# Moving two sets of 128x128 transposes of an attention kernel from TensorE to 32x32 block transposes on VectorE and transfers inside SBUF

## The chip, the cores and the metric

The kernel runs on one core of one Trainium2 chip. The metric is the device time of one execution in microseconds (us). A core has five engines with a queue of instructions each: TensorE (PE, matrix multiplications; its weight loads are shown apart as PEld), VectorE (DVE), ScalarE (ACT), GpSimd (POOL) and SyncE (SP), which here only issues transfers. Every engine works through its queue in order. SBUF is the working memory of 128 partitions, PSUM the memory that TensorE writes its results into.

## The reference

Two layers on 16 graphs of 1024 nodes with 256 features. Only the first layer is touched. Its attention uses the same values as queries, keys and values, in 8 heads of 32 features:

```python
h = jnp.maximum(_layernorm(x, axis=-1), 0.0)
normed = layer_norm(h, gamma1, beta1)
qkv = normed.reshape(b_, n_, H, HD).transpose(0, 2, 1, 3)      # H = 8, HD = 32
scores = jnp.einsum('bhqd,bhkd->bhqk', qkv, qkv) * scale
attn = jax.nn.softmax(jnp.where(mask, scores, -jnp.inf), axis=-1)
out = jnp.einsum('bhqk,bhkd->bhqd', attn, qkv)
out = out.transpose(0, 2, 1, 3).reshape(b_, n_, d_)
h2 = h + out
y = layer_norm(h2, gamma2, beta2)
x = x + h2 + (jax.nn.gelu(y @ W1 + b1) @ W2 + b2)
# second layer: h = relu(layernorm(x)); attention over all features of h,
# with logits h W a_12 W^T h^T + ..., then elu(h W_1 + attention h W_2); x = x + that
```

All of it is computed in float32.

## The kernel before

The batch has 16 graphs; the text calls one graph a batch (b). The whole program is unrolled, and the order of the instructions on every engine is the order in which the program writes them (the last lines of `fast_path` fix it). That order is made by seven streams, each a generator that names the place of its next piece in units of a batch; the loop near line 1487 always takes the earliest piece. `stream_a` writes the attention of batch b at places b to b+1, `stream_c` prepares the values of batch b at b-0.70 to b-0.25, and `stream_b` writes the rest of batch b (the two matrix products of the first layer, then all of the second layer) from b+0.99 on, beside the attention of batch b+1. A clock counts the TensorE time written so far. `defer(us, f)` holds back a piece of another engine until the clock has moved on by that much, so that it stands in its engine's queue where its operands should be ready. `turns` is a list of TensorE transposes that are asked for; `make_turns` writes them at the start of the next unit of attention.

Attention works in units (half of the queries qh, group g of 4 heads, tile kt of 128 keys), 32 to a batch. `scores` multiplies keys by 512 queries, both read from `kT`, a tile with the four heads of a group in the four groups of 32 partitions, features along the partitions and nodes along the columns. Each product has 32 rows and 64 columns of the array, so eight lie side by side. VectorE adds the mask (line 1000), ScalarE takes the exponential (line 1007), and one unit later `weigh` multiplies the values `va` (nodes along the partitions) by it (line 1022). After 8 key tiles the result `o` has head and feature along its partitions and 512 queries along its columns. In batch 0 half of the mask is added by TensorE.

Two sets of transposes are concerned:

- `turn(i)` in `prologue` (line 817): `va` of 256 nodes, nodes along the partitions, becomes `kT`. Four 128x128 transposes on TensorE into the PSUM tile `ptk` (line 822), then one copy by ScalarE (line 825). Four times a batch.
- `finish` (line 951): VectorE copies `o` to `os` (line 1031), TensorE transposes it in four blocks into `ptos` (line 958), VectorE multiplies by the inverse of the softmax sum `rl` (line 960), POOL adds to `h` (line 964). Four times a batch, for each (qh, g). `invert` makes `rl` when all units are done that a half needs.

When `finished` counts both groups of a half, `prepare` may compute the layer norm of two tiles of `h` (statistics on VectorE, a power on POOL at line 744, normalising on VectorE), `turn` in `rest` transposes them (`pty`, line 1143), `expand` multiplies by W1 and `contract` by W2. In `rest`, chunks 0 and 1 belong to the first half of the nodes, 2 and 3 to the second.

SP issues all transfers in the written order: loads of masks (line 585), of x (lines 784 and 1108), transposing transfers of the masks (line 902) and the stores of the output (line 1321).

Of the kernel before, what the change touches and what calls it, by code (L numbers as in the profile page):

```python
# [17 lines left out]
P = 128  # L18
# [477 lines left out]
def fast_path(  # L496
# [54 lines left out]
    ep = pool("ep", 6)  # L551
    denp = pool("denp", 2)
    lp1 = pool("lp1", 6)
# [220 lines left out]
    def prologue(b, st):  # L774
# [42 lines left out]
        def turn(i):  # L817
# [8 lines left out]

        steps = [
# [6 lines left out]
            lambda i: turns.append((1, lambda: turn(i))),  # L834
# [116 lines left out]
    def finish(b, qh, g, rl, ready, os):  # L951
        h = hs[b]
        run_deferred(ready)
        finished[b, qh] = finished.get((b, qh), 0) + 1
        clock[0] += 0.5
        pt = ps_tile([P, TPH, P], f"ptos_{b}_{g}_{qh}")
        for t in range(TPH):
            nc.tensor.transpose(pt[:, t, :], os[:, t * P : (t + 1) * P], ident)
        ot = tmpp.tile([P, TPH, GH, HD], F32, tag="w2", bufs=5, name=f"ot_{b}_{g}_{qh}")
        nc.vector.tensor_mul(  # L960
            ot, pt.rearrange("p t (j d) -> p t j d", d=HD), rl.unsqueeze(3).to_broadcast([P, TPH, GH, HD])
        )
        ho = h[qh][:, :, g * P : (g + 1) * P]
        nc.gpsimd.tensor_add(ho, ho, ot.rearrange("p t j d -> p t (j d)"))  # L964

    def attention(b, st):
        va, kT = st["va"], st["kT"]
        den = denp.tile([P, NQH, NT, H], F32, tag="den", name=f"den_{b}")


        def scores(qh, g, kt):
            qs = slice(qh * QW, (qh + 1) * QW)
# [11 lines left out]
            for j in range(GH):  # L984
                r = slice(j * HD, (j + 1) * HD)
                for c in range(0, P, P // 2):
                    nc.tensor.matmul(  # L987
                        sc[j // 2][c : c + P // 2, j % 2, :],
                        kT[r, g, kt * P + c : kt * P + c + P // 2],
                        kT[r, g, qs],  # L990
                        start=j >= by_pe,
                        stop=True,
                    )
# [23 lines left out]
        def weigh(qh, g, kt, es):  # L1017
            if kt == 0:
                acc[g, qh] = pso.tile([P, QW], F32, tag="o", name=f"o_{b}_{g}_{qh}")
            o = acc[g, qh]  # L1020
            for j in range(GH):
                nc.tensor.matmul(  # L1022
                    o[j * HD : (j + 1) * HD, :],
                    va[:, kt, (g * GH + j) * HD : (g * GH + j + 1) * HD],
                    es[j // 2][:, j % 2, :],
                    start=(kt == 0),
                    stop=(kt == NT - 1),
                )
            if kt == NT - 1:
                c = os[g, qh] = tmpp.tile([P, QW], F32, tag="w2", bufs=5, name=f"os_{b}_{g}_{qh}")  # L1030
                nc.vector.tensor_copy(c, o)
                if qh == NQH - 1:
                    close(qh, g)

        def close(qh, g):
            turns.append((1, lambda: finish(b, qh, g, *rl[g, qh], os[g, qh])))

        def invert(qh, g):
            r = smallp.tile([P, TPH, GH], F32, tag="rl", name=f"rl_{b}_{g}_{qh}")
            ts, hs_ = slice(qh * TPH, (qh + 1) * TPH), slice(g * GH, (g + 1) * GH)  # L1040

            def f():
                nc.vector.tensor_tensor(r, den[:, 0, ts, hs_], den[:, 1, ts, hs_], op=ALU.add)
                nc.vector.reciprocal(r, r)

            rl[g, qh] = r, defer(2.5, f)

        units = [(qh, g, kt) for qh in range(NQH) for g in range(NG) for kt in range(NT)]
        for u in units:
# [6 lines left out]
            if qh == NQH - 1 and kt % TPH == TPH - 1:  # L1056
                invert(kt // TPH, g)
                if kt < NT - 1:
                    close(kt // TPH, g)
# [40 lines left out]
    def rest(b, st, tails):  # L1100
# [232 lines left out]
        yield from tails[b]()  # L1333
        while finished.get((b, 1), 0) < NG:
# [3 lines left out]
        hid[1] = yield from expand(1)  # L1338
# [87 lines left out]
    def stream_b():  # L1426
        for b in range(B):
# [3 lines left out]
            for us, others in states[b]["rest"]:  # L1431
                clock[0] += us
                done += us
                if others is None:

                    if places[1] is None:
                        make_turns()
                    else:
# [122 lines left out]
```

## Time and profile before

| | |
|---|---|
| time, median of three runs | 3422.67 us (3421.1 to 3423.42) |
| the profiled execution | 3422.06 us, of which the span from first to last instruction is 3420.3 us |
| busy: TensorE, VectorE, ScalarE, POOL | 98%, 82%, 60%, 26% of the span |
| granted TensorE clock | 0.999 of full speed |
| transfers | 145.22 MB, the transfer engines 16% busy |
| one batch in the steady part (1500 to 1714 us) | 214 us: TensorE 212.96, VectorE 180.40, ScalarE 131.97, POOL 56.70 busy |

Lines of the profile name the source line, the engine, the tiles written and read, and, for groups, the count, the total busy time, the mean duration of one in nanoseconds and the idle time of the engine in front of them. A wait is shown as engine, instruction, what released it, total us, number of times, longest. The time of one instruction on TensorE contains its pipeline, so that the distance between the starts of two blocks is a better measure of what a block costs than its own length.

### The profile page before, as it was taken

To read this page: it belongs to the slowest core of one execution; us is meant where nothing else is said; L and a number is where in the kernel's file an instruction comes from. 1 tells how busy PE (TensorE), PEld (TensorE's weight loads), DVE (VectorE), ACT (ScalarE), POOL (GpSimd) and SP (SyncE) were. 2 spreads that over 40 slices of the span, in tenths; PEclk is the share of its full clock that TensorE was granted. 3 is DMA by queue.
4 is the path that set the end of the run, shared out by engine and by line. 5 is a ranking of instruction groups with operands and counts; after the bars stand their busy time and mean duration, and the time that the engine had idled before them with its cause. 6 is when DMAs were issued, how large, how long until landed. Compare 5 with 4: busy or idle time off the path is not lost. (4 is left out here: it accounts for less than half of the span.)

```text
span 3420.3 us, 114618 instructions
## 1 busy us (share of the span) xinstructions
PE 3356.2 (98%) x49790; PEld 1603.4 (47%) x49790; DVE 2799.1 (82%) x5427; ACT 2061.6 (60%) x5192; POOL 880.6 (26%) x1038
## 2 busy tenths in 40 slices
PE   6899999999999999999999999999999999999998
PEld 1244444444444444444444444444444444444477
DVE  6788888888888978888888887888879788897854
ACT  6665666656566565666656656666665655666532
POOL 3422232222323222232222312223222232321120
PEclk9999999999999999999999999999999999999999
DMA  4111202112011121111211112120211211111000
GB/s 135 45 39 40 57 17 54 39 47 56 20 46 39 48 54 34 40 31 48 54 39 48 25 50 45 42 56 18 52 39 48 55 26 40 39 48 42 8 19 14
DMA packets 157471, 145.22 MB, mean 42 GB/s; under 512 B 81056, under 2 KB 116256, under 8 KB 156960
## 3 DMA queue, kind: packets, MB, share of 16 engines
q1 hardware_dynamic: 156672, 137.56, 15.8%
q8 instruction: 392, 6.42, 0.8%
q14 instruction: 119, 0.97, 0.1%
q10 hardware_dynamic: 288, 0.26, 0.0%
HBM read 104.21 MB, written 16.78 MB: 35 GB/s over the span
## 5 line engine op out<-in xcount | busy, mean ns | idle before, releaser
L1007 ACT ACTIVATE e<-e 128x512 f32<-128x512 f32 x1984 | 1224.8, 619 | 960.5 <-DVE e L1000 958.1
L1000 DVE TENSOR_TENSOR e<-s,mk 128x1024 f32<-128x1024 f32 x992 | 1168.1, 1218 | 195.2 <-PE s L987 192.7
L987 PE MATMUL s<-kT 32*64 32x512 f32 x8192 | 579.5, 615 | 1.1 <-DVE e L1000 0.9
L1022 PE MATMUL o<-e,va 128*32 128x512 f32 x4096 | 557.5, 606 | 1.3 <-ACT e L1007 1.3
L572 PE MATMUL lg<-fT,uT 128*32 128x256 f32 x7680 | 454.1, 379 | 0.0
L572 PE MATMUL pa<-gw,e 128*32 128x258 f32 x7552 | 453.3, 380 | 0.0
L572 PE MATMUL ph<-yT,w 128*32 128x256 f32 x7808 | 451.0, 379 | 0.0
L572 PE MATMUL po<-w,hid 128*32 128x256 f32 x7680 | 438.9, 379 | 0.0
L1007 ACT ACTIVATION_READ_ACCUMULATOR e<-e 128x1 f32 x1984 | 371.2, 187 | 0.0
L572 PEld LDWEIGHTS ph<-yT,w 128*32 128x32 f32 x7808 | 255.5, 110 | 213.0 <-issue 55.7
L572 PEld LDWEIGHTS lg<-fT,uT 128*32 128x32 f32 x7680 | 257.3, 110 | 200.5 <-issue 43.3
L572 PEld LDWEIGHTS pa<-gw,e 128*32 128x32 f32 x7552 | 252.3, 110 | 206.6 <-issue 56.5
L572 PEld LDWEIGHTS po<-w,hid 128*32 128x32 f32 x7680 | 249.6, 110 | 209.6 <-issue 62.8
L1022 PEld LDWEIGHTS o<-e,va 128*32 128x32 f32 x4096 | 83.6, 108 | 424.6 <-issue 198.9
L1267 DVE SCALAR_TENSOR_TENSOR e<-lg,gw,mk 128x256 f32<-128x256 f32 x512 | 221.7, 474 | 64.2 <-PE lg L572 37.4
L1273 ACT ACTIVATE e<-e,shift 128x512 f32<-128x512 f32 x256 | 182.2, 715 | 141.5 <-DVE e L1272 103.8
L964 POOL TENSOR_TENSOR h<-h,ot 128x512 f32<-128x512 f32 x64 | 84.7, 1323 | 697.8 <-DVE ot L960 697.8
L917 POOL TENSOR_TENSOR odd<-mk,mq 128x512 bf16<-128x512 fp8e5 x192 | 233.3, 1216 | 100.2 <-DVE uneven L924 100.2
L1170 DVE TENSOR_TENSOR hid<-ph,b1c 128x512 f32<-128x512 f32 x256 | 173.6, 683 | 77.8 <-PE ph L572 67.8
L1272 DVE SCALAR_TENSOR_TENSOR e<-e 128x512 f32<-128x512 f32 x256 | 209.5, 818 | 8.8
L987 PEld LDWEIGHTS s<-kT 32*64 32x64 f32 x8192 | 122.7, 130 | 161.0 <-issue 105.0
L744 POOL TENSOR_TENSOR rs_c<-ve_c,mhalf 128x2 f32<-128x2 f32 x64 | 44.5, 695 | 477.4 <-DVE ve_c L742 378.1
(135 smaller groups left out, 3477.0 us busy)
## 6 DMA issues: line engine op xcount, KB each, us to landing
adj<-in_adj_dram SPq DMA_DIRECT2D x248, 256.0 KB, 3.6
h<-in_x_dram SPq DMA_DIRECT2D x64, 256.0 KB, 4.0
xb<-in_x_dram SPq DMA_DIRECT2D x128, 128.0 KB, 2.3
out_dram<-z SPq DMA_DIRECT2D x128, 128.0 KB, 1.7
adj<-in_adj_dram SPq DMA_DIRECT2D x4, 512.0 KB, 7.0
mk<-mq SPq DMA_TRANSPOSE x128, 3.8
w<-in_L_gnn_W_dram SPq DMA_DIRECT2D x2, 1024.0 KB, 8.7
wo<-in_L_gnn_W_dram SPq DMA_DIRECT2D x2, 256.0 KB, 9.8
```

The lines of the kernel that those rows point to most:

```text
L572: nc.tensor.matmul(out[c : c + HD], lhsT[:, c : c + HD], rhs, start=start, stop=stop)
L744: nc.gpsimd.tensor_tensor(rs, ve, mhalf[:, :nt], op=ALU.pow)
L917: nc.gpsimd.tensor_tensor(odd.rearrange("p (u v x) -> p u v x", u=2, v=2), key.rearrange("p (u v x) -> p u v x", u=2, v=2), query.rearrang ...
L964: nc.gpsimd.tensor_add(ho, ho, ot.rearrange("p t j d -> p t (j d)"))
L987: nc.tensor.matmul(sc[j // 2][c : c + P // 2, j % 2, :], kT[r, g, kt * P + c : kt * P + c + P // 2], kT[r, g, qs], start=j >= by_pe, stop= ...
L1000: nc.vector.tensor_tensor(e, masked, mb, op=ALU.add)
L1007: nc.scalar.activation(e[:, j], masked[:, j], AF.Exp, scale=SCALE, accum_out=den[:, qh, kt, n : n + 1])
L1022: nc.tensor.matmul(o[j * HD : (j + 1) * HD, :], va[:, kt, (g * GH + j) * HD : (g * GH + j + 1) * HD], es[j // 2][:, j % 2, :], start=(kt = ...
L1170: nc.vector.tensor_tensor(hid[:, f0 : f0 + 2, :], ph, b1c[:, f0 : f0 + 2].unsqueeze(2).to_broadcast([P, 2, CW]), op=ALU.add,)
L1267: nc.vector.scalar_tensor_tensor(e[:, j, :], lg[:, j, :], gw[:, kt, D : D + 1], st[c // 2][:, kt // 2, qs, kt % 2], op0=ALU.add, op1=ALU.add,)
L1272: nc.vector.scalar_tensor_tensor(e, e, ALPHA, e, op0=ALU.mult, op1=ALU.max)
L1273: ready = defer(2.5, lambda: nc.scalar.activation(e, e, AF.Exp, bias=shift))
```

## The change

In batches 1 to 15, `turn` is replaced by `turn_half`, once for 512 nodes: VectorE transposes `va` in blocks of 32x32 into a new tile `blocks`, and 16 transfers on the SP queue, of 32 partitions and 32 KB each, put the blocks into `kT`. The columns of `kT` then have another order inside a half: node k of tile t stands at column 4k + t in place of 128t + k. `scores` reads it through `by_tile`, so that keys and queries are read with a step of four elements (16 bytes) in these batches. Batch 0 keeps its transposes on TensorE and its order of columns.

In all batches, `finish` is gone. VectorE transposes `o` from PSUM in blocks of 32x32 into a new tile `block`, 16 transfers of 32 partitions and 16 KB each put them into `os`, which then has the queries along its partitions, and POOL multiplies by `rl` and adds to `h`. The transfers are written 2.0 us of the clock after the transpose, POOL's part 14.0 us (second half) or 4.5 us (first half) after the point where it is asked for.

In `rest`, `expand(1)` is written ahead of the wait for the second half's attention instead of behind it. While `stream_b` waits with no attention left, the clock now moves on. The pool of the exponentials has 5 buffers in place of 6, `os` has 4 in place of 5.

```diff
-    ep = pool("ep", 6)
+    ep = pool("ep", 5)
     denp = pool("denp", 2)
+    turnp = pool("turnp", 1)
...
+        def turn_half(i):
+            if i % 2 == 0:
+                return
+            qh = i // 2
+            x = turnp.tile([P, D // HD, HD, TPH], F32, tag="blocks", name=f"xk_{b}_{qh}")
+            nc.vector.transpose(
+                x.rearrange("p n i t -> p n t i"),
+                va[:, qh * TPH : (qh + 1) * TPH, :].rearrange("p t (n d) -> p n t d", d=HD),
+            )
+            xs = x.rearrange("p (g n) i t -> p g n (i t)", g=NG)
+
+            def move():
+                for n in range(GH):
+                    for a in range(GH):
+                        nc.sync.dma_start(
+                            kT[n * HD : (n + 1) * HD, :, qh * QW + a * P : qh * QW + (a + 1) * P],
+                            xs[a * HD : (a + 1) * HD, :, n, :],
+                        )
+
+            defer(2.5, move)
...
-            lambda i: turns.append((1, lambda: turn(i))),
+            turn_half,
...
-    def finish(b, qh, g, rl, ready, os):
-        h = hs[b]
-        run_deferred(ready)
-        finished[b, qh] = finished.get((b, qh), 0) + 1
-        clock[0] += 0.5
-        pt = ps_tile([P, TPH, P], f"ptos_{b}_{g}_{qh}")
-        for t in range(TPH):
-            nc.tensor.transpose(pt[:, t, :], os[:, t * P : (t + 1) * P], ident)
-        ot = tmpp.tile([P, TPH, GH, HD], F32, tag="w2", bufs=5, name=f"ot_{b}_{g}_{qh}")
-        nc.vector.tensor_mul(
-            ot, pt.rearrange("p t (j d) -> p t j d", d=HD), rl.unsqueeze(3).to_broadcast([P, TPH, GH, HD])
-        )
-        ho = h[qh][:, :, g * P : (g + 1) * P]
-        nc.gpsimd.tensor_add(ho, ho, ot.rearrange("p t j d -> p t (j d)"))
...
+        order = "p g (h t k) -> p g h t k" if b == 0 else "p g (h k t) -> p g h t k"
+        by_tile = kT.rearrange(order, h=NQH, k=P)
+
+        def keys(r, g, kt, c):
+            return by_tile[r, g, kt // TPH, kt % TPH, c : c + P // 2]
+
+        def queries(r, g, qh):
+            return by_tile[r, g, qh]
...
-                        kT[r, g, kt * P + c : kt * P + c + P // 2],
-                        kT[r, g, qs],
+                        keys(r, g, kt, c),
+                        queries(r, g, qh),
...
-                c = os[g, qh] = tmpp.tile([P, QW], F32, tag="w2", bufs=5, name=f"os_{b}_{g}_{qh}")
-                nc.vector.tensor_copy(c, o)
+                x = turnp.tile([P, GH, TPH, HD], F32, tag="block", name=f"xo_{b}_{g}_{qh}")
+                nc.vector.transpose(x, o.rearrange("p (t a i) -> p a t i", t=TPH, a=GH))
+                c = os[g, qh] = tmpp.tile([P, GH, TPH, HD], F32, tag="w2", bufs=4, name=f"os_{b}_{g}_{qh}")
+
+                def move():
+                    for j in range(GH):
+                        for a in range(GH):
+                            nc.sync.dma_start(c[a * HD : (a + 1) * HD, j], x[j * HD : (j + 1) * HD, a])
+
+                defer(2.0, move)
                 if qh == NQH - 1:
-                    close(qh, g)
-
-        def close(qh, g):
-            turns.append((1, lambda: finish(b, qh, g, *rl[g, qh], os[g, qh])))
+                    close(qh, g, 14.0)
+
+        def close(qh, g, us):
+            def f():
+                finished[b, qh] = finished.get((b, qh), 0) + 1
+                c = os[g, qh].rearrange("p j t d -> p t j d")
+                ho = hs[b][qh][:, :, g * P : (g + 1) * P].rearrange("p t (j d) -> p t j d", d=HD)
+                nc.gpsimd.tensor_mul(c, c, rl[g, qh].unsqueeze(3).to_broadcast([P, TPH, GH, HD]))
+                nc.gpsimd.tensor_add(ho, ho, c)
+
+            defer(us, f)
...
                 if kt < NT - 1:
-                    close(kt // TPH, g)
+                    close(kt // TPH, g, 4.5)
...
         yield from tails[b]()
+        hid[1] = yield from expand(1)
         while finished.get((b, 1), 0) < NG:
             yield 0.0, None
         prepare(b, st, 2)
         load(2)
-        hid[1] = yield from expand(1)
         ask(turn, 2)
...
                     if places[1] is None:
                         make_turns()
+                        clock[0] += 0.5
```

More of the change, by code (lines that the diff above doesn't have):

```diff
@@ L968, in attention @@
         den = denp.tile([P, NQH, NT, H], F32, tag="den", name=f"den_{b}")
+        order = "p g (h t k) -> p g h t k" if b == 0 else "p g (h k t) -> p g h t k"
[4 more added lines that the diff above has]
+            return by_tile[r, g, qh]
         def scores(qh, g, kt):
-            qs = slice(qh * QW, (qh + 1) * QW)
             sc = [
@@ L1029, in weigh @@
             if kt == NT - 1:
-                c = os[g, qh] = tmpp.tile([P, QW], F32, tag="w2", bufs=5, name=f"os_{b}_{g}_{qh}")
-                nc.vector.tensor_copy(c, o)
-                if qh == NQH - 1:
-                    close(qh, g)
-        def close(qh, g):
-            turns.append((1, lambda: finish(b, qh, g, *rl[g, qh], os[g, qh])))
+                x = turnp.tile([P, GH, TPH, HD], F32, tag="block", name=f"xo_{b}_{g}_{qh}")
[6 more added lines that the diff above has]
+                defer(2.0, move)
+                if qh == NQH - 1:
+                    close(qh, g, 14.0)
[7 more added lines that the diff above has]
+            defer(us, f)
         def invert(qh, g):
-            r = smallp.tile([P, TPH, GH], F32, tag="rl", name=f"rl_{b}_{g}_{qh}")
-            ts, hs_ = slice(qh * TPH, (qh + 1) * TPH), slice(g * GH, (g + 1) * GH)
+            r = rl[g, qh] = smallp.tile([P, TPH, GH], F32, tag="rl", name=f"rl_{b}_{g}_{qh}")
+            ts, heads = slice(qh * TPH, (qh + 1) * TPH), slice(g * GH, (g + 1) * GH)
             def f():
-                nc.vector.tensor_tensor(r, den[:, 0, ts, hs_], den[:, 1, ts, hs_], op=ALU.add)
+                nc.vector.tensor_tensor(r, den[:, 0, ts, heads], den[:, 1, ts, heads], op=ALU.add)
                 nc.vector.reciprocal(r, r)
-            rl[g, qh] = r, defer(2.5, f)
+            defer(2.5, f)
         units = [(qh, g, kt) for qh in range(NQH) for g in range(NG) for kt in range(NT)]
```

## The prediction

> **What bounds the kernel now.** I read the page's first part, then what TensorE waits for, then its timeline inside one batch, then the groups of instructions that the change touches, and last the SP queue.
>
> ```profile
> PE 3356.2 (98%) x49790; PEld 1603.4 (47%) x49790; DVE 2799.1 (82%) x5427; ACT 2061.6 (60%) x5192; POOL 880.6 (26%) x1038
> ```
>
> TensorE is busy for 3356 of 3420 us. A busy TensorE need not be a full one, so the waits and the timeline have to confirm it.
>
> ```profile
> PE ptk L822 <- POOL va L815: 20.0, 6, 15.0
> PE ptos L958 <- DVE os L1031: 7.6, 14, 1.1
> PE ptos L958 <- ACT gw L1249: 5.0, 13, 0.4
> PE pty L1143 <- DVE y L748: 1.6, 2, 1.3
> PE o L1022 <- ACT e L1007: 1.3, 1, 1.3
> ```
>
> Columns: total us, number of waits, longest. In all of the span TensorE waits for next to nothing. The 20.0 us of ptk lie in batch 0: asked for the window from 220 us on, this wait is gone. Batch 0 keeps its transposes, so these 20 us stay.
>
> ```profile
> 1736.55 1.05 PE L572 MATMUL pf<-wo,fT 128*32 128x256 f32 x16
> 1737.52 0.66 PE L822 MATMUL ptk<-ident,va 128*128 128x128 f32 x4
> 1738.11 1.11 PE L987 MATMUL s<-kT 32*64 32x512 f32 x16
> 1739.15 1.06 PE L1022 MATMUL o<-e,va 128*32 128x512 f32 x8
> 1740.04 3.67 PE L572 MATMUL pa<-gw,e 128*32 128x258 f32 x64
> 1743.64 1.28 PE L987 MATMUL s<-kT 32*64 32x512 f32 x16
> ```
>
> Start and duration of each block. The blocks follow each other without a hole: a unit of attention is 1.04 us of scores (1738.11 to 1739.15) and 0.89 us of weighing. So the order on TensorE sets the end, and an instruction that leaves it shortens the kernel.
>
> ```profile
> L964 POOL TENSOR_TENSOR h<-h,ot 128x512 f32<-128x512 f32 x64 | 84.7, 1323 | 697.8 <-DVE ot L960 697.8
> L960 DVE TENSOR_TENSOR ot<-ptos,rl 128x512 f32<-128x512 f32 x64 | 44.0, 687 | 2.1 <-PE ptos L958 0.2
> L1031 DVE COPY os<-o 128x512 f32<-128x512 f32 x64 | 43.6, 681 | 0.0
> L825 ACT COPY kT<-ptk 128x512 f32<-128x512 f32 x64 | 36.7, 573 | 11.0 <-PE ptk L822 11.0
> ```
>
> ```profile
> SPq L1321 <- DVE z L1320: 1487.4, 80, 74.5
> 1543.59 0.34 SPq L1321 DMA_DIRECT2D out_dram<-z  x1
> out_dram<-z SPq DMA_DIRECT2D x128, 128.0 KB, 1.7
> ```
>
> SP stands for most of the time at a store that waits for VectorE (up to 74.5 us), issues it in 0.34 us, and it lands 1.7 us later. SP therefore follows VectorE's order closely.
>
> [...] the trace's copy of 512 elements (681 ns) is my price for it. [...] After the change two operands have a step of exactly 16 bytes; no row of this trace has one[...]. [...] the trace has 1.7 us (128 KB store) and 2.3 us (xb loads).
>
> **The change part by part.**
>
> *TensorE loses* four transposes per group: 4 groups of ptk in batches 1 to 15 (60) and 4 of ptos in all 16 (64), 124 groups. One costs 0.59 us to the start of the next block, after a gap of 0.11 us (pf, 0.86 us per 16, would end at 1737.41). Where scores follow another block directly the gap is about 0.13 us (64 pa take 3.48 us from 1740.04, the scores start at 1743.64), and that gap comes back. Net 0.57 us, times 124 = 71 us. With them go the ptos waits, 7.6 + 5.0 = 12.6 us. Together 83 us.
>
> *ScalarE loses* 60 copies of 573 ns (34 us), not the bound.
>
> *VectorE loses* 64 x (0.681 + 0.687) = 87.5 us. It gains 64 transposes of 512 elements, at 0.68 us = 43.5 us, and 30 of 1024 elements (two a batch). For these the nearest row is the mask addition, 1.22 us for 1024 elements; they write with a step of 16 bytes, so up to twice that. I take 2.4 us: 72 us. Net +28 us, 2827 us or 84% of the shorter span: still not the bound. But a transpose of 2.4 us stands in front of the mask additions of one unit, whose chain (two additions 2.4 us, the exponentials 3.2 us) nearly fills the 5.5 to 6.5 us between units. Between 0 and 1 us of TensorE each, 0 to 30 us; I take 5.
>
> *POOL gains* 64 multiplications at the price of the addition, 1.32 us: 85 us, 26% to 29%. Hidden, as POOL's own idle time (698 us before L964 alone) covers it. Its new wait is for transfers: behind it stand the powers for the normalisations, which VectorE needs.
>
> *SP gains* 32 transfers a batch for kT (15 batches) and 64 for os: 1504, against about 700 now. At 0.34 to 0.53 us of issue (the store above; ten loads at the start take 5.3 us), I take 0.42: a move of 16 holds SP for 6.7 us, and 1504 hold it for 630 us, a fifth of the span. Behind a move wait mask loads and stores, none due within 7 us. The bytes (32 MB on 145) are nothing: the engines are 16% busy.
>
> *kT* is needed about a quarter of a batch (50 us) after the last half is turned; 0.7 to 2.4 us of VectorE, 6.7 and 2 us fit. TensorE must now see up to eight transfer counters at the first scores: an extra semaphore instruction takes 51 ns in this trace; up to 32 of them in 15 batches, 0 to 24 us, mostly behind running matmuls; I take 4.
>
> *The attention outputs*: from the last matmul to h it was 0.68 + 0.66 + 0.69 + 1.32 = 3.4 us; now 0.68 + 6.7 + 1.7 + 1.32 + 1.32 = 11.7 us, which the hand-set 14 us just admits. For the second half of a batch expand(1) (7.3 us of TensorE, some 11 with the units between) moves in front of the wait. This hides the transfers, but uses up what stood between prepare(2) and turn(2): statistics 1.5, power 0.7 and normalising 0.84 us, 3.2 us with hand-overs, must now fit beside one half contraction (1.75 us) or two. Late is y: 0 to 1.5 us a batch, 0 to 24 us; I take 6. In the last batch nothing else runs, so all 3 us show.
>
> *ep 6 to 5, w2 5 to 4*: nothing. A unit uses two e tiles, and the tile reused is one whose weighing stands on TensorE before the scores that refill it.
>
> *Strided operands of the scores*: in batches 1 to 15 keys and queries have a step of 16 bytes. One element of the fp32 stream enters in about 0.88 us / 512 = 1.7 ns, [...] so I take 0. Bounds: below, 0, as it removes no work; above, a halved stream, 0.88 us per unit in 480 units, 422 us; the weights alone (130 ns a load, once exposed) 62 us.
>
> Sum: 83 - 5 - 4 - 6 - 3 = 65 us. Against the profiled execution (3422.06 us, span 3420.3 and 1.8 around it; the median of 3422.67 is no different): 3357, say **3355 us**, own range 3335 to 3390.
>
> **Rivals.**
> 1. *The strided read costs (slower).* Scores take more than 1.04 us per unit in batches 1 to 15. [...] Against: [...] the operand is read elsewhere at this pace without a wait. It decides from 67 / 480 = 0.14 us per unit; at half of the bound 3355 + 211 = 3566, at the full one 3777.
> 2. *The weights' share only, or VectorE and y at their upper ends.* 62 us, or 25 + 20 + 18: 3355 + 45 = 3400, most of the gain is given back.
> 3. *Late moves.* SP runs behind, POOL stands at a transfer, VectorE waits for POOL's power, TensorE for both. It needs 67 / 16 = 4.2 us a batch; at 7 us (one further move in front) 3355 + 112 = 3467. Against: every entry of SP waits for VectorE in VectorE's own order, and expand(1) gives slack.
> 4. *The transposes were no bound* and TensorE only stops elsewhere: no change. Against: the timeline has no holes.
>
> **Numbers.** Forecast 0.50; rival 2 0.12; no change 0.05; rival 1 0.25; rival 3 0.08. A measurement of this kernel tells 0.2% (7 us) from no change. Faster 0.62, same 0.05, slower 0.33. Range 3325 to 3530: it holds rival 3 and the smaller half of rival 1, and leaves out the larger half (0.14) and little below. As both signs are in it, the forecast's own range is the one above.
>
> **What would show it.** Right: ptos and ptk gone after batch 0; scores still 1.04 us a unit; TensorE's waits under 30 us; VectorE's transposes of 0.7 and at most 2.4 us; POOL's multiplications early enough. Wrong: scores longer in batch 1 than in the unmasked part of batch 0, a wait of pty for y above 1.5 us a batch, VectorE idle for POOL, or SP issues of 1 us.

## The result, and the profile after

| | before | after |
|---|---|---|
| time, median | 3423.05 us (3421.1 to 3425.37) | 4137.72 us (4131.18 to 4138.52) |
| the profiled execution, its span | 3422.06 us, 3420.3 us | 4138.52 us, 4136.7 us |
| granted TensorE clock | 0.999 | 0.965 |
| TensorE at half clock | 12 us | 290 us |

After is 1.2083 times before (95% interval 1.2062 to 1.2104): 715 us slower, where 67 us faster was forecast. 3355 us and the range up to 3530 us are both missed.

The page of the changed kernel first: busy time by engine, then groups of instructions (count, busy us, mean ns, idle time of the engine before them and who ended it).

```profile
PE 3818.2 (92%) x49294; PEld 1609.8 (39%) x49294; DVE 2851.0 (69%) x5393; ACT 2036.3 (49%) x5132; POOL 952.0 (23%) x1102
...
L1001 PE MATMUL s<-kT 32*64 32x512 f32 x8192 | 1103.3, 1086 | 253.9 <-DVE e L1014 253.7
L1036 PE MATMUL o<-e,va 128*32 128x512 f32 x4096 | 563.7, 621 | 0.0
...
L1001 PEld LDWEIGHTS s<-kT 32*64 32x64 f32 x8192 | 192.8, 196 | 487.2 <-DVE e L1014 315.2
L593 DVE TENSOR_SCALAR mq<-adj 128x512 fp8e5<-128x512 int32 x248 | 96.8, 421 | 403.3 <-DMA adj<-in_adj_dram 403.3
...
L1062 POOL TENSOR_TENSOR os<-os,rl 128x512 f32<-128x512 f32 x64 | 67.3, 1052 | 1172.1 <-DMA os<-xo 856.6
```

The same two groups in the kernel before:

```profile
L987 PE MATMUL s<-kT 32*64 32x512 f32 x8192 | 579.5, 615 | 1.1 <-DVE e L1000 0.9
L592 DVE TENSOR_SCALAR mq<-adj 128x512 fp8e5<-128x512 int32 x248 | 93.9, 420 | 3.8 <-DMA adj<-in_adj_dram 3.8
```

TensorE issues 496 matmuls fewer and is busy for 462 us more. All of that and more stands in the scores: 1086 ns for one where the kernel before took 615, while the weighing, in the line after the scores, hardly changed (557.5 us before). The second thing to see is in the line of the mask conversion `mq`: VectorE stood 403.3 us in front of it, waiting for mask loads from memory; before it stood 3.8 us.

TensorE's waits (total us, times, longest):

```profile
PE s L1001 <- DVE e L1014: 253.7, 42, 15.4
PE pty L1172 <- DVE y L749: 22.9, 17, 3.9
PE ptk L823 <- POOL va L816: 18.6, 4, 15.6
```

The waits for `ptos` are gone, as forecast, and that for `ptk` is the old one of batch 0. In their place the scores wait for the mask addition, in stretches of up to 15 us. Inside one batch (start, duration), a unit that waits for nothing:

```profile
1802.19 0.66 PE L1248 MATMUL ptf<-ident,ft 128*128 128x128 f32 x4
1802.77 2.09 PE L1001 MATMUL s<-kT 32*64 32x512 f32 x16
1804.80 1.06 PE L1036 MATMUL o<-e,va 128*32 128x512 f32 x8
1805.68 3.64 PE L573 MATMUL po<-w,hid 128*32 128x256 f32 x64
```

From the start of the scores to the next block it is now 2.03 us; it was 1.04. One of the long stalls, seen from SP, which issues the transfers (start, time to issue them, how many):

```profile
1891.71 10.70 SPq L842 DMA_DIRECT2D kT<-xk  x16
1902.46 11.00 SPq L1051 DMA_DIRECT2D os<-xo  x16
1913.56 1.00 SPq L586 DMA_DIRECT2D adj<-in_adj_dram  x2
1914.61 1.24 SPq L924 DMA_TRANSPOSE mk<-mq  x1
```

from VectorE:

```profile
1917.30 0.43 DVE L593 TENSOR_SCALAR mq<-adj 128x512 fp8e5<-128x512 int32 x1 [17.99 <-DMA adj<-in_adj_dram]
1917.95 0.43 DVE L593 TENSOR_SCALAR mq<-adj 128x512 fp8e5<-128x512 int32 x1 [0.23 <-DMA adj<-in_adj_dram]
1918.30 2.35 DVE L1014 TENSOR_TENSOR e<-s,mk 128x1024 f32<-128x1024 f32 x2
```

and from TensorE:

```profile
1919.57 3.20 PE L1001 MATMUL s<-kT 32*64 32x512 f32 x16 [14.56 <-DVE e L1014]
1922.70 1.60 PE L1036 MATMUL o<-e,va 128*32 128x512 f32 x8
```

Read together: two moves of 16 transfers hold SP for 21.7 us. The load of two mask tiles is written behind them and leaves only at 1913.56. VectorE has reached the conversion of that mask, runs nothing else in the 17.99 us before it, and has the mask addition of the next unit behind the conversion. So TensorE stands for 14.6 us for a mask addition that has nothing to do with the mask that is late: the addition starts at 1918.30, 0.35 us after the conversion of the late mask, which has yet to pass through a transposing transfer. The load itself is not slow: mask loads land 3.6 us after their issue, in median, in both kernels; this one was issued late. The first scores afterwards take 3.20 us in place of 2.09. Their second half stands once more, for the second mask addition of the pair, which ends at 1920.65. The half clock of this stretch is not the reason: a unit is recorded as two rounds of matmuls, and the rounds start 0.98 us apart here as in the unit at 1802.77, at full clock.

### The profile page after: what moved, and what is told of

The parts are those of the page before. It is cut to its first block, busy times and chain, and to the rows that moved or that the text cites. A ratio compares the mean times of both kernels' runs of the same rounds, so it can differ in the third digit from the quotient of the medians.

```text
span 4136.7 us, 115685 instructions
## 1 busy us (share of the span) xinstructions
PE 3818.2 (92%) x49294; PEld 1609.8 (39%) x49294; DVE 2851.0 (69%) x5393; ACT 2036.3 (49%) x5132; POOL 952.0 (23%) x1102
## 5 line engine op out<-in xcount | busy, mean ns | idle before, releaser
L1001 PE MATMUL s<-kT 32*64 32x512 f32 x8192 | 1103.3, 1086 | 253.9 <-DVE e L1014 253.7
L1001 PEld LDWEIGHTS s<-kT 32*64 32x64 f32 x8192 | 192.8, 196 | 487.2 <-DVE e L1014 315.2
L593 DVE TENSOR_SCALAR mq<-adj 128x512 fp8e5<-128x512 int32 x248 | 96.8, 421 | 403.3 <-DMA adj<-in_adj_dram 403.3
L1062 POOL TENSOR_TENSOR os<-os,rl 128x512 f32<-128x512 f32 x64 | 67.3, 1052 | 1172.1 <-DMA os<-xo 856.6
L573 PEld LDWEIGHTS lg<-fT,uT 128*32 128x32 f32 x7680 | 248.5, 111 | 221.2 <-issue 67.2
L939 POOL TENSOR_TENSOR odd<-mk,mq 128x512 bf16<-128x512 fp8e5 x192 | 223.8, 1169 | 111.2 <-DVE uneven L946 111.2
(134 smaller groups left out, 3403.5 us busy)
```

The source lines that it names most:

```text
L573: nc.tensor.matmul(out[c : c + HD], lhsT[:, c : c + HD], rhs, start=start, stop=stop)
L593: nc.vector.tensor_scalar(m[:, i * QW : (i + 1) * QW], a, 0.0, NEG8, op0=ALU.is_le, op1=ALU.mult, saturate=False)
L939: nc.gpsimd.tensor_tensor(odd.rearrange("p (u v x) -> p u v x", u=2, v=2), key.rearrange("p (u v x) -> p u v x", u=2, v=2), query.rearrang ...
L1001: nc.tensor.matmul(sc[j // 2][c : c + P // 2, j % 2, :], keys(r, g, kt, c), queries(r, g, qh), start=j >= by_pe, stop=True,)
L1062: nc.gpsimd.tensor_mul(c, c, rl[g, qh].unsqueeze(3).to_broadcast([P, TPH, GH, HD]))
```

## The experiments

They were made in five steps: the operand, the queue of transfers, the transfers themselves, the place of the work on VectorE, and a last wait. Ratios are to the kernel before, with the 95% interval; a kernel without an interval ran once.

### The operand alone

**stride_in_before** is the kernel before, whose ScalarE copy writes `kT` in the changed order of columns; no transfer and no transpose of VectorE is in it.

```diff
-            nc.scalar.copy(kT[:, :, i * CW : (i + 1) * CW], pt)
+            if b == 0:
+                nc.scalar.copy(kT[:, :, i * CW : (i + 1) * CW], pt)
+            else:
+                spread_out = kT.rearrange("p g (h k t) -> p g h t k", h=NQH, k=P)
+                nc.scalar.copy(
+                    spread_out[:, :, i // 2, i % 2 * TPC : (i % 2 + 1) * TPC],
+                    pt.rearrange("p g (j k) -> p g j k", k=P),
+                )
...
-                        kT[r, g, kt * P + c : kt * P + c + P // 2],
-                        kT[r, g, qs],
+                        by_tile[r, g, kt // TPH, kt % TPH, c : c + P // 2],
+                        by_tile[r, g, qh],
```

> The kernel before with one edit: ScalarE's copy of the transposed values writes the columns of kT in the changed order, and keys and queries of batches 1 to 15 are read with a step of 16 bytes. No transfer is added. If the step is what lengthens the scores (1.04 to 2.03 us from start to start in the changed kernel), they do so here too, and the time is 3423 + 480 x 0.99 = about 3898 us. Rival, that the scores are longer because the added transfers take the memory of the operands: 1.04 us as before, about 3423 us.

Measured: 3855.67 us beside 3423.32, 432 us more. The groups of its page:

```profile
L996 PE MATMUL s<-kT 32*64 32x512 f32 x8192 | 1046.0, 1080 | 1.4 <-DVE e L1009 1.4
L996 PEld LDWEIGHTS s<-kT 32*64 32x64 f32 x8192 | 178.4, 195 | 159.5 <-issue 103.4 <-DVE mq L592 11.6 <-DVE z L1329 6.2
```

No new wait stands here and the clock is 0.999: the loss is the length of the scores. They are busy for 466 us more; a part comes back because other waits shrink behind them (those of `ptos` fall from 12.6 to 1.6 us), which the 3898 us expected had left out. **strided_queries** and **strided_keys** are the same kernel with only one of the two operands read with the step (the last two lines of the diff, one at a time).

> As stride_in_before, but only the moving operand (the queries) of batches 1 to 15 is read with a step of 16 bytes; the keys are read contiguously from the same tile, so that keys stand beside the mask of other nodes and the result differs from the reference. If the moving stream carries the cost, scores take about 2 us a unit and the time is 3840 to 3860 as with both; if the weights carry it, about 3423.

> The counterpart: only the stationary operand (the keys, 64 columns a load) has the step, the queries are contiguous and stand beside the mask of other nodes, so the result differs from the reference. If the moving stream carries the cost, scores take at most 0.1 us more a unit (one load of 195 in place of 130 ns in the open) and the time is 3423 to 3470; if the weights carry it, about 3850.

Measured: 3828.41 us and 3451.21 us beside 3423.34. The 512 queries that stream through the array cost 405 us, the keys that are loaded as weights 28 us, and the two add up to the 432. Keys alone raise a weight load from 130 to 195 ns and leave the scores at 643 ns.

### The queue in front of the masks

**no_stride** is the change with another order in its tiles: VectorE transposes a half in two instructions of 512 elements, `kT` has its old order inside a half, and keys and queries are contiguous. The moves are the same 16 transfers.

```diff
-            x = turnp.tile([P, D // HD, HD, TPH], F32, tag="blocks", name=f"xk_{b}_{qh}")
-            nc.vector.transpose(
-                x.rearrange("p n i t -> p n t i"),
-                va[:, qh * TPH : (qh + 1) * TPH, :].rearrange("p t (n d) -> p n t d", d=HD),
-            )
+            x = turnp.tile([P, GH, NG, TPH, HD], F32, tag="blocks", name=f"xk_{b}_{qh}")
+            for g in range(NG):
+                nc.vector.transpose(
+                    x[:, :, g],
+                    va[:, qh * TPH : (qh + 1) * TPH, g * P : (g + 1) * P].rearrange(
+                        "p t (n d) -> p n t d", d=HD
+                    ),
+                )
...
-            return by_tile[r, g, qh]
+            return kT[r, qh, g]
```

**masks_on_act** is the change as it stands, with the mask loads issued by ScalarE's queue (`nc.scalar.dma_start(a, ...)` at line 586). **both_mended** has both edits.

> The changed kernel with contiguous operands: the transfers put runs of 128 bytes at the usual columns of kT (16 transfers a half as before, four times as many pieces), the scores read without a step. If the step is the cause, scores are back at 1.04 us and the time is about 4138 - 475 = 3663 us, with the waits of the mask additions for late masks still there (250 us or more). If the transfers are the cause, the scores stay near 2 us and the time near 4138.

> The changed kernel with the 248 mask loads issued by ScalarE in place of SP; step kept. If the 254 us in which TensorE waits for the mask additions come from mask loads standing behind two moves of 16 transfers (11 us each) on SP, VectorE's 403 us of waiting for adj go, and the time is 3850 to 3890. Rival, that the moves hold the transfer engines and not the queue of the issuer: the loads land as late as before, 4138.

> No step and mask loads issued by ScalarE together. If the two costs are separate and all there is, the time is 4138 - 475 - 270 = about 3390 us, below before by 20 to 50 us. If a third cost is hidden (y late for its transpose, POOL waiting for transfers), it stays above 3423.

Measured: 3912.77, 3958.33 and 3601.33 us (both_mended 1.0524, 1.0506 to 1.0542). Without the step the scores take 642 ns, but VectorE's idle time in front of `mq` rises to 438.4 us, the waits of the scores to 363.0 and the half clock to 478 us; 225 us are won of the 432, where 475 were expected. Half clock also costs more here: in the trace of the changed kernel it lengthens a contiguous matmul (the weighing takes 1060 ns at half clock and 604 at full clock, means), but not one of the scores with the step (1111 ns at either). With the masks on ScalarE's queue the wait of `mq` falls from 403.3 to 13.8 us and that of the scores to 12.5, and yet only 179 us are won: ScalarE now stands itself. Its waits, and one of them in order of time:

```profile
ACT e L1021 <- DVE e L1014: 1204.1, 407, 5.6
ACT e L1021 <- DMA os<-xo: 191.8, 19, 13.6
```

```profile
1824.68 3.54 ACTq L586 DMA_DIRECT2D adj<-in_adj_dram  x2
1828.33 0.63 ACT L1021 ACTIVATE e<-e 128x512 f32<-128x512 f32 x1 [13.07 <-DMA os<-xo]
```

The second line of waits is new. No exponential reads `os`. ScalarE's waiting instruction stands directly in front of the mask load: in the trace it is released at 1824.59 by a transfer of `os` that lands, and the load is issued at 1824.68. `os` moves and mask loads count on the same eight semaphores (in the trace of the changed kernel 128 transfers of `os` on each, and 24 to 39 mask loads), so the likeliest reading is that a load stands for a counter that other transfers use too. That was not tried by itself, and neither was what keeps both_mended 178 us above the kernel before.

**os_alone** keeps `turn` on TensorE in all batches and changes the attention outputs only, so that moves never come two in a row.

```diff
-            turn_half,
+            lambda i: turns.append((1, lambda: turn(i))),
-        order = "p g (h t k) -> p g h t k" if b == 0 else "p g (h k t) -> p g h t k"
+        order = "p g (h t k) -> p g h t k"
```

> The changed kernel with the turning of the next values left on TensorE as in the kernel before: no kT moves, no step; the attention outputs by VectorE and transfers as changed. TensorE loses 64 groups and their waits, about 49 us. If the late masks come from two moves standing one behind the other on SP (kT's and os's, 22 us), the masks come in time here, TensorE's wait for mask additions falls below 100 us and the time is 3390 to 3480. If a single move of 11 us is enough, the wait stays near 360 us and the time near 3700.

Measured: 3725.68 us, 302 us more than before, `mq` idle 271.1 us in 62 waits of up to 12.6 us, scores waiting 165.1 us. One move is enough to make the masks late; the thought that two in a row were needed fell.

**masks_ahead** loads every mask one step earlier (`adjp` 2 to 4 buffers, `ep` 5 to 4 to make room) on the base of no_stride, and asks for the second half's `y` only after `contract(0)`. **split_moves** issues each move in four pieces of four transfers, 3 us apart, with the late asking and the 4 buffers of `ep` too; the diff is that of its attention outputs, the values alike.

```diff
-                defer(2.0, move)
+                for j in range(GH):
+                    defer(2.0 + 3.0 * j, lambda j=j: move(j))
```

> The changed kernel with contiguous operands, mask loads written one step earlier (four buffers in place of two, the exponentials have four), and the second half's transpose asked for after the first contraction instead of ahead of it; all transfers on SP. If late masks and late y are what is left over the 83 us gained, the time is 3350 to 3410; if SP's moves cost something else too, it stays above 3423.

> Complete: contiguous operands, later asking, and the moves written in four pieces of 4 transfers, 3 us of the clock apart, so that mask loads stand between the pieces (exponentials 4 buffers, blocks 2). If a move's length in one piece is the harm, DVE's wait for masks falls from 438 us to below 100 and the time is 3370 to 3450. If SP is simply too full in the part of a batch where masks are loaded, the wait stays above 200 us and the time above 3550.

Measured: 3700.6 us (1.0814, 1.0796 to 1.0833) and 3671.42 us (1.0723, 1.0706 to 1.0741). The idle time at `mq` is still 185.5 and 232.5 us, though in split_moves 33 of the 64 moves of `os` still left as 16 transfers in one piece. Both help by some 210 to 240 us against no_stride and neither removes the cause.

### One transfer in place of sixteen

**one_transfer** is no_stride with each move replaced by a single transfer of the same bytes, which leaves every row in its partition. **one_transfer_late_turn** adds the late asking for `y`.

```diff
-                    for j in range(GH):
-                        for a in range(GH):
-                            nc.sync.dma_start(c[a * HD : (a + 1) * HD, j], x[j * HD : (j + 1) * HD, a])
+                    nc.sync.dma_start(c, x)
...
+        yield from contract(0, hid[0])
         ask(turn, 2)
...
-        yield from contract(0, hid[0])
```

> The same without the later asking: the second half's transpose is asked for right behind its statistics, as in the change. The difference to one_transfer_late_turn is the price of the lost distance between prepare(2) and turn(2): 16 to 24 us if the waits of pty for y (23 to 42 us seen) come from there, none if they came from SP.

> Contiguous operands, the second half's transpose asked for after the first contraction, and each move of 16 transfers replaced by one transfer of the same bytes that keeps every row in its partition; the blocks then stand in the wrong partitions and the result differs from the reference. Waits, bytes and the chain to POOL stay, only SP's 11 us a move are gone. If SP's hold is the whole of the remaining loss, the masks are in time, y too, and the time is 3340 to 3365 (3423 - 83 and a few us). If the chain through transfers and POOL costs by itself, it stays above 3390.

Measured: 3462.06 us (1.0114, 1.0097 to 1.0131) and 3454.58 us (1.0103, 1.0086 to 1.012). The bytes, the work of VectorE and POOL and the two operands are those of no_stride, and 451 us are gone; VectorE stands 7.1 us in front of `mq` in one_transfer. What cost them is the number of instructions that SP has to issue. The packets, the pieces that the transfer engines move, are halved too (171005 for 337196), but a mask load that lands 3.7 us after its issue (no_stride, median; 3.6 in the kernel before) is not held by packets, and a transfer cut into four times as many pieces (no_stride's `kT` against that of the change) holds SP for 0.61 us in place of 0.595, in median. Asking later for `y` brings 7 us, which the spread of the runs does not tell from nothing (3457.9 to 3464.9 and 3450.9 to 3465.6 us). But the 65 us of gain do not come either. Where one_transfer_late_turn still waits (TensorE, then VectorE in the same stretch):

```profile
1752.55 3.67 PE L573 MATMUL pa<-gw,e 128*32 128x258 f32 x64
1758.89 3.12 PE L1000 MATMUL s<-kT 32*64 32x512 f32 x16 [2.68 <-DVE e L1013]
1761.94 1.94 PE L1035 MATMUL o<-e,va 128*32 128x512 f32 x8
```

```profile
1752.88 1.18 DVE L743 TENSOR_SCALAR ve_b<-mv_b 128x2 f32<-128x2 f32 x1
1753.98 0.86 DVE L1293 SCALAR_TENSOR_TENSOR e<-lg,gw,mk 128x256 f32<-128x256 f32 x2
1754.88 1.64 DVE L1298 SCALAR_TENSOR_TENSOR e<-e 128x512 f32<-128x512 f32 x1
1756.44 1.29 DVE L834 STREAM_TRANSPOSE xk<-va 128x512 f32<-128x512 f32 x2
1757.66 2.31 DVE L1013 TENSOR_TENSOR e<-s,mk 128x1024 f32<-128x1024 f32 x2
```

Once a batch there is a stretch in which VectorE has no idle time. The two transposes (1.29 us) stand in it directly in front of the mask addition that the scores wait for. After the wait the scores take 3.12 us in place of 1.11: the clock is halved (the weighing behind them takes 1.94 us in place of 1.07), and their second half stands for the second of the two mask additions.

### The place of the transposes on VectorE

**kt_alone_split** is the kernel before with only the values transposed by VectorE: contiguous, the 16 transfers in 8 pieces of two, 2 us apart; attention outputs stay on TensorE, and the exponentials have 4 buffers in place of 6. **turns_spread** is one_transfer_late_turn with the two transposes 3 and 6 us later in the written order and their transfer at 8.5 us in place of 2.5, **no_key_transposes** has them left out, and **kt_alone_spread** is kt_alone_split with them 4 and 10 us later and the pieces from 12.5 us on; its diff against kt_alone_split is shown.

```diff
-            for g in range(NG):
+            def turn_group(g):
                 nc.vector.transpose(
...
+            for g in range(NG):
+                defer(4.0 + 6.0 * g, lambda g=g: turn_group(g))
...
             for m in range(8):
-                defer(2.5 + 2.0 * m, lambda m=m: move(m // 2, m % 2 * 2))
+                defer(12.5 + 2.0 * m, lambda m=m: move(m // 2, m % 2 * 2))
```

> The kernel before with only the next values turned by VectorE: contiguous operands, transfers in eight pieces of 2, the attention outputs still transposed by TensorE. TensorE loses 60 groups, 34 us. With the 50 us of slack of kT and short pieces on SP the masks should be in time: 3390 to 3400, below before. If 32 added transfers a batch delay the masks even in pieces of 2, at or above 3423.

> The kernel of one_transfer_late_turn (contiguous operands, one transfer for each move with rows left in their partition, so its result differs) with VectorE's two transposes of a half of the values not issued together in front of a mask addition, but 3 and 6 us later in the written order, and their transfer at 8.5 us. Theory: what is left of the loss (3454.6 us where 3340 to 3357 was summed) comes from a stretch of each batch in which VectorE has no idle time: the two transposes (1.29 us) stand in front of the mask addition, the scores wait 2.7 us, and the clock of TensorE is halved for some us after it. Then the wait of the scores for the mask additions falls from 39 us to under 20 us and the time to 3405 to 3435 us. Rival: the stretch is full whatever the order, and what is moved comes back a unit later: 3445 to 3460 us, waits of 30 us or more.

> The kernel of one_transfer_late_turn with VectorE's transposes of the values left out: the transfer carries a constant tile, so keys and queries are constants and the result differs. Theory: with 41 us of VectorE's work gone from the full stretch the scores wait for mask additions under 15 us, and the time is 3385 to 3420 us; what then still stands above 3357 is not the transposes. Rival: VectorE's work has no share in it (late transfers, the order of the units or the clock alone): 3445 to 3460 us.

> The kernel of kt_alone_split (only the values transposed by VectorE, moves in 8 pieces of 2 transfers, all else as in the kernel before) with the two transposes 4 and 10 us later in the written order and the pieces from 12.5 us on. Theory: the holes in front of the scores and of the transposes of attention outputs (some 40 us) shrink, 3400 to 3425 us, the first version that is not slower than the kernel before. Rival: the full stretch moves only, 3430 to 3440 us.

Measured: kt_alone_split 3436.51 us (1.004, 1.0026 to 1.0055), turns_spread 3418.84 us (0.9987, 0.9981 to 0.9994), no_key_transposes 3418.8 us (0.9987, 0.9979 to 0.9995), kt_alone_spread 3403.5 us (0.9942, 0.9926 to 0.9959). The same instructions a few microseconds later, with their transfers, are worth 36 us in one kernel and 33 in the other; to leave them out altogether is worth no more than to place them well. kt_alone_spread is the one version here that puts all data in its right place and is faster than the kernel before, by 20 us of the 34 that 60 groups of transposes should give. Its waits:

```profile
PE ptos L985 <- ACT gw L1275: 10.5, 14, 0.8
PE ptos L985 <- DVE os L1057: 7.3, 12, 1.2
PE s L1013 <- DVE e L1026: 3.8, 5, 1.3
PE s L1013 <- DMA kT<-xk: 2.6, 1, 2.6
```

Those of `ptos` were there before (5.0 and 7.6 us). VectorE stands 6.0 us in all for mask loads: pieces of two transfers leave gaps in SP's queue. **three_of_four_spread** then turns three of the four attention outputs of a batch in the same manner, in 8 pieces of two transfers, 2 us apart; the fourth, which the feed-forward part waits for, stays on TensorE.

> The kernel of kt_alone_spread with three of the four attention outputs of a batch turned by VectorE as well, as in the change, but their 16 transfers issued in 8 pieces of 2 from 2 us on, each 2 us later than the one before; the fourth output of a batch, which the feed-forward part waits for, stays with TensorE; 4 buffers w2 for 5. Theory: with pieces of two transfers (1.2 us of SP) no mask is late, and 48 x 0.57 = 27 us of TensorE's transposes go, less what comes back as waits for mask additions: 3375 to 3400 us. Rival: VectorE's full stretch is the bound there by now, and TensorE's saving only turns into a wait of the scores once a batch, as in turns_spread: 3400 to 3425 us, waits of the scores for mask additions above 20 us. If masks are late again (VectorE idle for them for more than 50 us): above 3430 us.

Measured: 3536.18 us (1.0336, 1.0319 to 1.0354), `mq` idle 121.2 us: masks are late again. SP in one batch of it:

```profile
1615.29 1.71 SPq L849 DMA_DIRECT2D kT<-xk  x2
1617.10 1.02 SPq L586 DMA_DIRECT2D adj<-in_adj_dram  x2
1618.16 1.19 SPq L1069 DMA_DIRECT2D os<-xo  x2
1619.40 1.29 SPq L849 DMA_DIRECT2D kT<-xk  x2
```

The pieces of two sets now fill each other's gaps, and SP has almost none left from 1613 to 1651 us. Pieces of two left the masks in time in kt_alone_spread, where SP had gaps, and do not here.

### The last wait

turns_spread and no_key_transposes agree within 0.1 us, with 23.7 and 24.9 us of waits for mask additions, once a batch. Both have the addition `ve_b` of the stretch shown above at 1.18 us once in each of 14 batches, where it usually takes 0.17; another in each of them takes 0.62, and that one does so in the kernel before too. In turns_spread VectorE and POOL show it so:

```profile
1532.29 1.18 DVE L743 TENSOR_SCALAR ve_b<-mv_b 128x2 f32<-128x2 f32 x1
```

```profile
1530.69 1.62 POOL L1064 TENSOR_TENSOR h<-h,os 128x512 f32<-128x512 f32 x1
1532.27 1.16 POOL L944 TENSOR_TENSOR odd<-mk,mq 128x512 bf16<-128x512 fp8e5 x1
```

It begins 0.02 us after POOL's comparison `odd` and ends with it. The long addition of the kernel before also ends with `odd`, but begins 0.56 us behind it; here POOL's new work stands in front of `odd`. **eps_on_pool** and **no_key_eps_on_pool** let POOL do that addition, in the two kernels just named.

```diff
-        nc.vector.tensor_scalar_add(ve, mv[:, :, 1], EPS)
+        e = nc.gpsimd if name[0] == "b" else nc.vector
+        e.tensor_scalar_add(ve, mv[:, :, 1], EPS)
```

> The kernel of turns_spread (contiguous operands, one transfer for each move with rows left in their partition, so its result differs; VectorE's transposes 3 and 6 us later) with the addition of epsilon to the variance of the second normalisation (128x2 elements, name ve_b) done by POOL in place of VectorE. Theory: in the full stretch of each batch this addition took 1.18 us in place of 0.17, and ended 0.03 us after POOL's comparison of masks in 14 of 14 cases: VectorE stood for POOL. On POOL it holds VectorE no longer, the wait of the scores for the mask addition falls from some 1.8 us a batch to 0.8 us or nothing, fewer stretches of half clock (now 61 us) follow: 3375 to 3408 us. Rival: the batch stays at 208.2 us, since a stall in each batch falls into the same place of the 3.413 us stretches in which the clock is set and costs half of one: 3413 to 3424 us, half clock above 45 us. Rival 2: the normalisation comes later by POOL's queue and the values with it, nothing is won: 3418 us or more with waits above 20 us.

> The same edit (the addition of epsilon on POOL) in the kernel of no_key_transposes, which leaves VectorE's transposes of the values out (keys and queries are constants, the result differs). Theory: with VectorE's wait for POOL gone and 41 us less of its work no wait of the scores is left and no half clock: 3355 to 3385 us, below eps_on_pool. If this kernel and eps_on_pool agree within 3 us again, VectorE's load by the transposes has no share, or both stay at 61 stretches of 3.413 us a batch (3413 to 3424 us); the half clock tells these two apart: above 45 us for the second.

Measured: 3373.49 us (0.9853, 0.9837 to 0.987) and 3373.68 us (0.9857, 0.984 to 0.9873). TensorE's waits in eps_on_pool:

```profile
PE s L573 <- ACT e L1025: 11.9, 21, 1.5
PE s L1005 <- DVE e L1018: 5.9, 5, 2.3
PE pty L1174 <- DVE y L750: 5.4, 1, 5.4
```

The place of one addition of two elements a partition was worth 45 us: 18 us of waits, and the stretches of half clock that followed them (61 us in turns_spread, 22 here). That no_key_eps_on_pool is no faster shows that the load of VectorE by the transposes has no share once they are placed well; its own expectation of 3355 to 3385 us holds, that it would lie below eps_on_pool does not. The rival, that the clock holds a batch at 208.2 us, fell: a batch takes 204.9 us here.

## Why the prediction was wrong, step by step

- **What bounds the kernel, and what TensorE loses.** Right. Counted from start to start, `ptk` and `ptos` cost 82 us before and 7 us in eps_on_pool, and the waits of `ptos` are gone. With the costs below taken away the time is 3373 us, 49 us under the kernel before, in the forecast's own range (3335 to 3390) and 18 us above the 3355. These 18 stand in the scores: 596 us from start to start, 30 more than before. Two units in each batch make most of it, one behind `pty` and one behind `pa`, with 2.02 and 1.76 us in place of 1.04 and 1.21, some 22 us in all. In eps_on_pool:

```profile
1627.95 2.09 PE L1005 MATMUL s<-kT 32*64 32x512 f32 x16
1629.97 1.06 PE L1040 MATMUL o<-e,va 128*32 128x512 f32 x7
```

The second half of such a unit starts only at 1628.96, released by VectorE's mask addition at 1628.91, and so no longer beside the first half; in the kernel before eight matmuls, four of each half, start within 0.05 us (from 1738.11 on). The table of waits does not count this, because the first half is still running. eps_on_pool leaves rows in the wrong partitions, so it supports the sum and is no kernel; and the addition of epsilon was not moved in the kernel before, where 14 of them take 0.62 us, so a part of the 49 us may not belong to the change.
- **"Strided operands … so I take 0."** This step failed, and the 1.7 ns an element that it rests on with it: 432 us when tried alone, 405 for the queries and 28 for the keys. The upper bound named there, 422 us for a halved stream, was close to the right value; a unit takes 0.98 us more against the 0.88 named. Rival 1 stood at its full size. The 1.7 ns misread the unit: the trace of the kernel before records it as two rounds of eight matmuls (1738.11 and 1738.59), each over the 512 columns, so that an element enters in about 0.48 us / 512 = 0.9 ns and not in 1.7, which is an estimate from these starts. With the step it takes 1.9 ns, at half clock as at full.
- **"I take 0.42 us issue: a move of 16 holds SP 6.7 us."** Mis-sized: 0.59 us is the median issue of a transfer, and a move holds SP for 10.9 us in median (10.0 to 12.4). The rows used as price were a store and loads over 128 partitions; these transfers cover 32.
- **"Behind a move wait mask loads and stores, none due within 7 us."** The step that failed for the second half of the loss. The mask loads are due sooner, and the one that waits for them is VectorE, which has mask additions of other masks behind the conversion. Loads one step ahead (masks_ahead) did not suffice. What of the loss stands above the full rival 1 (4138 - 3777 = 361 us) is for the most part this: 254 us of waits of the scores, and some 59 us in units whose second half comes late, as above. Half clock adds some 33 us, an estimate: of its 290 us TensorE stands for 177, 47 are scores with the step, which it does not lengthen, and half of the other 65 is lost. The wait of `pty` has 17 us more than was taken. Its share is not additive with the step's: the step costs 432 us alone, but only 225 come back when it is taken out of the change, since the shorter scores wait longer and are slowed by half clock.
- **Rival 3, late moves.** The place was right (SP behind), the victim was not. POOL does stand for the moves (856.6 us), and nothing comes of it; the one to watch was VectorE at the next load in SP's queue.
- **Transposes in front of mask additions, "0 to 30 us; I take 5".** The step named the right cause; 36 us measured in one_transfer_late_turn, some 16 of them waits (39.2 to 23.7 us) and about as much the half clock behind them (95 to 61 us of it).
- **"POOL gains 64 multiplications … Hidden."** Right for POOL (1052 ns each where 1320 were taken), wrong for VectorE: on the new schedule a small addition of VectorE ends with POOL's work in the fullest stretch, 45 us. No term of the sum had it.
- **Attention outputs and `y`.** 6 us taken; the wait of `pty` is 22.9 us in the changed kernel, 1.3 us a time, at the upper end of the 0 to 1.5 us named; what asking later is worth (7 us) lies within the spread of the runs.
- **VectorE's transposes**, 0.68 and 2.4 us taken, an estimate from the copy and the mask addition: 0.71 and 2.08 us, right. Two of 512 elements without the step take 0.68 us each (no_stride, median). `kT` came in time: the scores wait for no transfer. The smaller buffers `ep` and `w2` were not tried by themselves.

The error behind the two large terms is one: an operation without a row in the trace was given the value of its nearest neighbour. For the step the bound was named and given a chance of 0.25; for the moves the next load behind them was taken to be due later than it is.

## What to carry to other kernels

A transfer costs its issuing queue an instruction each (0.59 us of SP here), and the queue's other customers pay: before a move of n transfers is put on a queue, multiply n by the issue time of that shape, find the next load in the queue, and ask what stands behind the engine that consumes it. A saving on the bounding engine reaches the end only if the helper engines are not full in that stretch (36 us lay there in one_transfer_late_turn), so read their timeline around the tightest wait, and place added work there last. A layout that makes TensorE read an operand with a step of 16 bytes is paid in every unit that reads it (2.03 us in place of 1.04 here); no_stride put the other order into the moves, which are made once, and the scores were back at 642 ns.

## What the runs showed of the hardware

- A moving operand of 512 fp32 elements with a step of 16 bytes takes twice the time, 2.03 us in place of 1.04 for a unit of 16 matmuls, and a weight load 195 ns in place of 130. Half clock does not lengthen these matmuls: the 224 that lie in it take 1111 ns in mean in the changed kernel, as do the 7440 at full clock, while the weighing goes from 604 to 1060 ns. ScalarE's copy that writes with the step takes 1101 ns for 573.
- A transfer inside SBUF over 32 partitions holds SP for 0.59 us, median, against 0.47 us for one over 128 partitions (one_transfer_late_turn, at 1667.38) and 0.34 us for a store over 128 partitions.
- The stretches of half clock in the trace of the changed kernel last 3.413 us or 2, 4 or 5 times as long (4, 4, 9 and 7 of them; one more is cut off by the end of the trace). In turns_spread 1.48 us of standing, from 1535.6 to 1537.1, came before one (window, its length, TensorE busy and instructions, granted clock, DMA):

```profile
1535.50:1537.00 1.50, 0.12 (x4) 1.00 0.00 0
1537.00:1541.00 4.00, 3.86 (x23) 0.66 0.00 0
1541.00:1545.00 4.00, 4.00 (x40) 0.50 0.34 134
```

  Over the trace of turns_spread this costs about as much as the waits themselves: TensorE works for 51 of the 61 us of half clock, so some 26 us are lost, an estimate, beside 23.7 us of waits. How long a standing it takes stays open: cut into steps of 3.413 us, on whose limits all changes of its clock lie, the trace of the changed kernel has half clock behind none of the 318 steps at full clock with less than 0.6 us of standing, behind 8 of the 52 with 0.6 to 2.4 us and behind all 17 with more.
- An addition of VectorE on two elements a partition lasted 1.18 us in place of 0.17 where it began 0.02 us after a comparison of POOL (turns_spread), and 0.62 us where the comparison had begun 0.56 us earlier (the kernel before). It ended 0.03 us after the comparison in all 14 cases of either kernel, and moving it to POOL won 45 us. Why the two end together was not shown.
